# A decoder layer on one NeuronCore: the shared expert's pieces spread anew over three stretches, and the experts begun two slots sooner

## The chip, the core and the metric

The kernel runs on one NeuronCore of a Trainium2 chip. Its engines each work through a queue of their own, in order: TensorE (PE) multiplies matrices into PSUM, VectorE (DVE) and ScalarE (ACT) work on tiles in SBUF and read PSUM, GpSimd (POOL) works on tiles and issues indirect DMAs, SyncE (SP) issues ordinary DMAs, and 16 DMA engines carry them out. They meet only through semaphores. The metric is device time of one launch in microseconds; smaller is better. The run used for the profile has a time of its own, which stands beside the median of the other runs below.

## What is computed

One decoder layer on x of shape (32, 256, 256), all in float32. Self-attention with 16 heads of 16 and a layer norm; cross-attention to a context of 120 rows, each head the difference of two softmaxes, and a layer norm; then a mixture of experts on the 8192 tokens, whose result is added to the tokens and normalised again. The part that matters here is the last:

```python
scores = jax.nn.sigmoid(x @ router_weight.T)                # 64 experts
_, top_idx = jax.lax.top_k(scores + expert_bias, 6)
# each expert takes at most CAP = 96 of its tokens, in order
hmid = gelu(einsum('ech,ehf->ecf', xs, w1))                 # 256 -> 128
y = einsum('ecf,efh->ech', hmid, w2)                        # 128 -> 256
out = zeros.at[token_of].add(y_pair)                        # weighted, scattered back
shared = gelu(x @ sw1.T) @ sw2.T                            # 256 -> 512 -> 256, every token
x = layernorm(x + out + shared)
```

The routed experts see at most 64 x 96 rows. The shared expert sees every token.

## The kernel before

**Two stages.** In the first, the 32 batch entries go through both attentions, the router and the dispatch, software-pipelined: every step of a batch entry has a place in a table (`plan`), keyed by an iteration number and a part of it (`pre`, `mm`, `post`), and line 1121's loop runs the iterations. The last step of a batch entry (`dispatch`, line 1070) scatters its token rows, by 12 indirect DMAs of POOL, to the DRAM buffer `slots`, where each expert has 96 rows. Ahead of it stand on PE `router` and `places` (line 1036, two small products that count the tokens ahead of each), and on DVE `route`, `keys` and `slots_of` (line 1060). For the last entries the steps lie closer: `router` in iteration 18 after the entry's cross-attention began, `places` in iteration 20, the dispatches from 21 to 25. `store` puts each entry's normalised tokens in DRAM twice: transposed in `x2T_d`, and as the start of `acc[0]`; `acc[1]` is cleared.

In the second stage (from line 1138) the 64 experts are taken as 32 pairs. A loop over slots emits the work; pair n has its number n = slot - START. In slot n PE transposes the pair's rows (`turn`), one slot on it does the first product (`up`), and another slot on the second (`down`). In the slot after that DVE weights the result into one of six tiles `ye` and POOL issues two indirect DMAs that add it to DRAM (`scatter`, line 1229): the first expert of the pair into `acc[0]`, the second into `acc[1]`. Two scatters into the same `acc` are not in flight together: the later one waits for the earlier one to land. The rows of the next pairs (`rows_of`, eight tiles `xs`) and their weights (`expert_weights`, ten tiles `four`) are loaded by SP as tiles come free: the rows of pair m wait for the `ye` of pair m - 8.

After the experts come the 16 blocks of 512 tokens (`Last`, line 1252), one step each: `fetch` loads both `acc`, `add` sums them on POOL, `stats` adds the shared expert's `y` on DVE and takes mean and variance, `scale` makes the factors on ACT and POOL, `put` normalises on ACT and stores. The engines' queues hold these parts in the order in which the loop emits them. The first `fetch` waits until every scatter has landed.

**The shared expert's pieces.** `shared` (line 242) is a Python generator. Each `next(pieces)` emits one piece and stops. After an opening piece that loads weights, there are four pieces for each block k: two that multiply block k with half of `sw1` each (call them f), with a gelu on ACT after each, and two that multiply block k - 1's gelu with `sw2` (call them q), each followed by a copy on ACT into the tile `y` of block k - 1. That is 64 pieces of work in all, in the order f f q q. What reads a piece's PSUM is held in `unread` and emitted by `settle()` at the next piece, so a gelu or copy stands on ACT's queue behind whatever was emitted in between. PSUM in the second stage has two double banks for f and four single banks for q and for the pairs (`Apart`, line 213). The loads of a block's tokens (`load`, line 245, four tiles `x2T`) are emitted on SP three blocks ahead.

Pieces are emitted in four stretches. In the first stage, one `next` at line 1125 and one in each of the iterations named on line 1131, counted from the start of the last entry's cross-attention. In the second, one in each slot before START, then in the slots in which line 1339 says so, and from END = START + 32 + 3 on one in each slot, two in each fourth slot:

```python
            if slot < START or slot < END and n % 3 < 2:
                pieces_on(1)
            elif slot >= END:
                pieces_on(1 if slot % 4 else 2)
            if slot >= END and (not 2 <= steps < NBLK + 2 or steps - 2 in whole):
```

The last line means that the step with block k's `stats` is emitted only once both q pieces of block k, and their copies, have been.

The first EARLY blocks keep their `y` in a tile of their own in the pool `ffn`, which is there in both stages (line 261). The other blocks' `y` lie in `ypool`, which is opened in the second stage over memory that the first stage used, so their first writes wait for the last readers of that memory; so do the first loads of weights and rows. At START - 2 the rows of the first six pairs are asked for, and in slot 1 their weights.

The order on each engine's queue is the order of emission (`InOrder`, line 163, writes it down as dependencies), so a piece emitted between two other steps is done between them.

Of the kernel before, what the change touches and what calls it, by code (L numbers as in the profile page):

```python
# [37 lines left out]
def tile_decoder_layer(  # L38
# [24 lines left out]
    B, T, _ = x.shape  # L63
# [167 lines left out]

    NQ = TB // P
    NBLK = NT // TB
    EARLY = min(3, NBLK)
    ys, whole, unread = {}, set(), []

    def settle():

        while unread:
            unread.pop()()  # L240

    def shared(ypool):
# [15 lines left out]
        def keep(k, q2, ps):  # L258
            if q2 == 0:
                tag = "y" if k >= EARLY else f"y{k}"  # L260
                bufs = None if k >= EARLY else 1
                ys[k] = ypool(k).tile([P, NQ, D], F32, tag=tag, name=tag, bufs=bufs)
# [59 lines left out]
    with ExitStack() as one:  # L322
# [777 lines left out]
        batches = [Batch(b) for b in range(B)]  # L1100
        ypools = []
        pieces = shared(lambda k: ypools[0] if k >= EARLY else ffns[0])

        def run(n, part):
            for _, f, args in sorted(plan.pop((n, part), ()), key=lambda step: step[0]):
                f(*args)

        def score_products(k):

            pairs = []  # L1110
            for kind, behind in ((Batch.weights, 10), (Batch.maxima, 0)):
                for bt in batches:
                    if any(0 <= k - 2 * t - behind < 8 for t in (bt.start, bt.cross)):
                        pairs.append(kind(bt, k))
            for n in range(2):
                for mms, _ in pairs:
                    for dst, lhsT, rhs in mms[2 * n : 2 * n + 2]:
                        pe.matmul(dst, lhsT=lhsT, rhs=rhs, start=True, stop=True)
            return [read for _, read in pairs]

        for n in range(min(plan)[0], max(plan)[0] + 1):
            if n == batches[-1].start + 13:
                early_end.close()
                ffns.append(ctx.enter_context(tc.tile_pool(name="ffn", bufs=2, side="right")))
                next(pieces)
            run(n, "pre")
            settle()
            for read in score_products(2 * n) + score_products(2 * n + 1):
                read()
            run(n, "mm")  # L1130
            if n - batches[-1].cross in (-5, -1, 3, 7, 9, 10, 11, 12, 13, 14, 15, 16, 17, 18, 19, 20):
                next(pieces)
            run(n, "post")
        settle()
# [3 lines left out]
    with ExitStack() as two:  # L1138
# [4 lines left out]
        small = two.enter_context(tc.tile_pool(name="small2", bufs=3))  # L1143
        ypool = two.enter_context(tc.tile_pool(name="ypool", bufs=NBLK - EARLY - 1))
        ypools.append(ypool)
        AHEAD = 6
        START = 7

        fours = itertools.count()

# [4 lines left out]
        def rows_of(n):  # L1155

            xs = wk.tile([CAP, 2, XPW], F32, name=f"xs{n % 8}", bufs=1)
            sp.dma_start(
                out=xs,
                in_=slots[2 * n * CAP : (2 * n + 2) * CAP, :].rearrange("(e s) d -> s e d", s=CAP),  # L1160
            )
            return xs

        def tokens_of(n):

            code = xs_of[n][:, :, D + NE]
            empty = small.tile([CAP, 2], F32, tag="empty", name="empty")
            dve.tensor_scalar(empty, code, 0.0, slot_f[:CAP, :], ALU.is_equal, ALU.mult)
            token = small.tile([CAP, 2], F32, tag="token", name="token")
            dve.tensor_scalar(token, code, -1.0, float(NT), ALU.mult, ALU.add)  # L1170
            idx = small.tile([CAP, 2], I32, name=f"idx{n % 12}", bufs=1)
            dve.tensor_add(idx, token, empty)
            return idx

        def expert_weights(n):

            wt = next_four([P, 2, D // P * F + D])
            sp.dma_start(out=wt, in_=w12[n])
            return wt
# [125 lines left out]
        last = [Last(k) for k in range(NBLK)]  # L1305
        END = START + NP + 3
        slot = steps = 0
        more = True

        def pieces_on(n):  # L1310
            nonlocal more
            for _ in range(n):
                if more:
                    more = next(pieces, "end") != "end"

        def fetch_for(n):
            if n < NP:
                xs_of[n] = rows_of(n)
                weights_of[n] = expert_weights(n)

        while more or steps < NBLK + 5:
            n = slot - START

            if 0 <= n - 1 < NP:
                pairs[n - 1].turned()
            if 0 <= n - 2 < NP:
                pairs[n - 2].gelu()
            if 0 <= n - 3 < NP:
                pairs[n - 3].scatter()
            if slot == 1:  # L1330
                for k in range(AHEAD):
                    weights_of[k] = expert_weights(k)
            if slot == START - 2:
                for k in range(AHEAD):
                    xs_of[k] = rows_of(k)
            if 0 <= n < NP:
                idx_of[n] = tokens_of(n)

            if slot < START or slot < END and n % 3 < 2:
                pieces_on(1)  # L1340
            elif slot >= END:
                pieces_on(1 if slot % 4 else 2)
            if slot >= END and (not 2 <= steps < NBLK + 2 or steps - 2 in whole):
                for part, behind in (
                    (Last.fetch, 0),
                    (Last.add, 1),
                    (Last.scale, 3),
                    (Last.put, 4),
                    (Last.stats, 2),
                ):  # L1350
                    if 0 <= steps - behind < NBLK:
                        part(last[steps - behind])
                steps += 1
            if 0 <= n < NP:
                pairs[n].turn()
            if 0 <= n - 1 < NP:
                pairs[n - 1].up()
            if 0 <= n - 2 < NP:
                pairs[n - 2].down()
                fetch_for(n - 2 + AHEAD)  # L1360
            slot += 1
# [62 lines left out]
```

## Time and profile before

| | |
|---|---|
| median of 7 runs | 1932.17 us (1929.36 to 1939.80) |
| the profiled execution's own time | 1926.0 us |
| its span, first to last instruction | 1924.3 us |
| granted TensorE clock, mean | 0.979 |

The busy time by stretches, from the trace, in us:

| stretch | PE | DVE | ACT | POOL | DMA engines, mean share |
|---|---|---|---|---|---|
| 0 to 1600: first stage but for its end | 1530.37 | 1118.19 | 938.73 | 985.75 | 0.15 |
| 1600 to 1643: end of the first stage | 41.01 | 13.74 | 16.55 | 34.58 | 0.17 |
| 1643 to 1671: up to the first scatter | 26.32 | 4.07 | 10.60 | 3.44 | 0.85 |
| 1671 to 1848: the pairs of experts | 167.70 | 52.23 | 40.70 | 90.18 | 0.69 |
| 1848 to 1924: the 16 blocks | 34.54 | 53.00 | 51.13 | 58.91 | 0.86 |

A stretch of 1643 to 1671 is 28 us long, so PE's 26.32 there means that it hardly paused. All instructions carry line 173, that of a helper, so tiles tell them apart: `two<-x2T,w_s` is an f piece (8 matmul instructions), `one<-w_s,gT` a q piece (16), `one<-ident,xs` the transposes of a pair, `one<-xsT,four` its first product, `one<-four,hT` its second, `acc<-ye,idx` a scatter, `slots<-xpt,slot` a dispatch.

In an engine's lines in order of time the columns are start and duration in us, engine, line, operation, written and read tiles with their shapes, how many instructions were merged, and in brackets the idle time of the engine before it and what is taken to have ended it. That last is inferred from semaphores and can name the wrong one.

### The profile page before, as it was taken

The numbers are of one execution on the slowest core, as the hardware profiler recorded it, in microseconds if no ns is written. First come the engines' busy times: TensorE is split into PE (matmuls) and PEld (weight loads), VectorE is DVE, ScalarE is ACT, GpSimd is POOL, SyncE is SP. The second block draws the span as 40 slices with busy tenths as digits, with TensorE's granted clock in tenths as the row PEclk, the third lists the DMA queues.
The fourth block names the chain that finished last, engine by engine and source line by source line (L and its number), as shares of the span: only waits on it lengthen the run. The fifth ranks groups of instructions, "written<-read, shape, count | busy, mean of one in ns | idle before, by whom it ended". The sixth has DMA issues, their size and how long they took to land. (4 is left out here: it accounts for less than half of the span.)

```text
span 1924.3 us, 44465 instructions
## 1 busy us (share of the span) xinstructions
PE 1799.9 (94%) x17800; PEld 1316.7 (68%) x17800; DVE 1241.2 (65%) x2749; ACT 1057.7 (55%) x1807; POOL 1172.9 (61%) x1242
## 2 busy tenths in 40 slices
PE   7999999999999999999999999999999879998973
PEld 4777777777777776777777777777777556676642
DVE  5566677777777777777777777777777534133246
ACT  1666666655556665555666655555666554222237
POOL 7444445666666666666666666666445658344567
PEclk9999999999999999999999999999999889999987
DMA  3070111111111111111111111111012012787477
GB/s 114 15 193 7 32 31 59 63 45 44 38 35 37 35 34 35 35 37 35 35 34 32 33 32 33 32 33 33 22 31 85 19 56 57 206 224 202 85 233 308
DMA packets 109550, 132.14 MB, mean 69 GB/s; under 512 B 33019, under 2 KB 94676, under 8 KB 109344
## 3 DMA queue, kind: packets, MB, share of 16 engines
q1 hardware_dynamic: 78832, 106.83, 17.9%
q0 software_dynamic: 25600, 13.02, 4.1%
q10 hardware_dynamic: 4912, 9.46, 1.3%
q8 instruction: 140, 2.29, 0.5%
q14 instruction: 66, 0.54, 0.1%
HBM read 74.62 MB, written 111.04 MB: 96 GB/s over the span
## 5 line engine op out<-in xcount | busy, mean ns | idle before, releaser
L173 DVE TENSOR_REDUCE pad_mx<-all 128x4 f32<-128x1024 f32 (+1 forms) x512 | 586.9, 1187 | 277.8 <-PE all L173 277.4
L173 ACT ACTIVATE pt<-all 128x512 f32<-128x512 f32 (+3 forms) x768 | 516.8, 740 | 273.9 <-PE all L173 216.8
L173 PE MATMUL all<-qT,kT 32*128 32x256 f32 (+1 forms) x4096 | 518.7, 390 | 37.7 <-POOL qT L173 34.7
L173 PE MATMUL all<-kT,qT 32*128 32x256 f32 (+1 forms) x4096 | 511.1, 388 | 5.1 <-DVE qkb L173 2.9
L173 PEld LDWEIGHTS all<-qT,kT 32*128 32x128 f32 (+1 forms) x4096 | 363.4, 182 | 162.0 <-issue 71.1
L173 POOL DMA_INDIRECT slots<-xpt,slot x384 | 385.4, 1004 | 95.0 <-issue 91.3
L173 PEld LDWEIGHTS all<-kT,qT 32*128 32x128 f32 x4096 | 365.9, 186 | 17.6 <-DVE qkb L173 3.3
L173 POOL TENSOR_TENSOR qT<-qT,mT 128x512 f32<-128x512 f32 x126 | 159.1, 1283 | 222.7 <-ACT mT L173 222.7
L173 PE MATMUL all<-w_qkv,xT 128*128 128x512 f32 (+1 forms) x512 | 184.1, 494 | 8.6 <-DMA xT<-in_xT 8.6
L173 ACT COPY ot<-all 128x512 f32<-128x512 f32 x192 | 112.1, 589 | 95.7 <-PE all L173 85.4
L173 POOL DMA_INDIRECT acc<-ye,idx x64 | 90.2, 1409 | 107.2 <-DMA acc<-ye,idx 33.9
L173 POOL TENSOR_SCALAR rs<-mv 128x2 f32<-128x2 f32 x64 | 14.2, 222 | 190.4 <-DVE mv L173 190.0
L173 PEld LDWEIGHTS all<-w_qkv,xT 128*128 128x128 f32 x512 | 94.1, 194 | 51.4 <-issue 43.9
L173 ACT COPY T<-all 128x512 f32<-128x512 f32 x128 | 73.1, 591 | 91.2 <-PE all L173 88.0
L173 PE MATMUL all<-pt,pad_xv 120*32 120x256 f32 x2048 | 119.1, 384 | 2.9 <-ACT pt L173 2.8
L173 PE MATMUL all<-pt,pad_v 128*32 128x256 f32 x2048 | 117.1, 381 | 0.0
L173 POOL TENSOR_TENSOR rc<-qkb,cosr 128x512 f32<-128x512 f32 x62 | 79.9, 1289 | 47.4 <-DVE qkb L173 46.4
L173 POOL TENSOR_TENSOR pad_qk<-rc,qkb 128x256 f32<-128x256 f32 x124 | 102.2, 845 | 2.7
L173 PE MATMUL all<-ident,ot 128*128 128x128 f32 x768 | 103.5, 278 | 0.0
L173 PE MATMUL one<-w_s,gT 128*128 128x256 f32 x416 | 95.0, 384 | 5.4 <-ACT gT L173 2.4
L173 PEld LDWEIGHTS all<-ident,ot 128*128 128x128 f32 x768 | 84.0, 142 | 21.4 <-ACT pt L173 13.4
L173 PEld LDWEIGHTS all<-pt,pad_xv 120*32 120x32 f32 x2048 | 63.5, 111 | 48.8 <-issue 6.8
(155 smaller groups left out, 2921.8 us busy)
## 6 DMA issues: line engine op xcount, KB each, us to landing
four<-in_w SPq DMA_DIRECT2D x32, 512.0 KB, 5.0
four<-acc SPq DMA_DIRECT2D x32, 512.0 KB, 6.2
xT<-in_xT SPq DMA_DIRECT2D x32, 256.0 KB, 3.5
xt<-in_x SPq DMA_DIRECT2D x32, 256.0 KB, 4.3
x2T_d<-T SPq DMA_DIRECT2D x32, 256.0 KB, 2.5
acc<-xpt SPq DMA_DIRECT2D x32, 256.0 KB, 2.6
acc<-zero SPq DMA_DIRECT2D x32, 256.0 KB, 3.1
x2T<-x2T_d SPq DMA_DIRECT2D x16, 512.0 KB, 6.3
```

Of the source, the lines that this page charges most:

```text
L173: ins = f(*args, **kwargs)
```

## The change

Four numbers and one condition change. EARLY goes from 3 to 4, so block 3's `y` gets a tile in `ffn`, and `ypool` has 11 tiles, not 12. In the first stage, iterations 17 to 20 take two pieces each, not one: 20 in place of 16. START goes from 7 to 5: five pieces, not seven, stand ahead of the first pair's slot, and the rows of the first pairs are asked for in slot 3, not 5. Between START and END a piece is emitted in each third slot (12 pieces), not in two of three (24). What is left, 28 calls in place of 18, comes from END on.

```diff
-    EARLY = min(3, NBLK)
+    EARLY = min(4, NBLK)
...
-            if n - batches[-1].cross in (-5, -1, 3, 7, 9, 10, 11, 12, 13, 14, 15, 16, 17, 18, 19, 20):
+            for _ in range(
+                (-5, -1, 3, 7, 9, 10, 11, 12, 13, 14, 15, 16, 17, 17, 18, 18, 19, 19, 20, 20).count(
+                    n - batches[-1].cross
+                )
+            ):
                 next(pieces)
...
-        START = 7
+        START = 5
...
-            if slot < START or slot < END and n % 3 < 2:
+            if slot < START or slot < END and n % 3 == 0:
                 pieces_on(1)
             elif slot >= END:
                 pieces_on(1 if slot % 4 else 2)
```

## The prediction

> **What bounds the kernel now.** The change touches the last 325 us, so I began with the busy times by stretches and then read each engine's lines in order of time. Two stretches of the pairs, whose columns are stretch, length, busy time and instruction count of PE, weight loads, DVE, ACT and POOL, then clock, DMA share and GB/s:
>
> ```profile
> 1671.00:1797.00 126.00, 116.70 (x619) 88.49 (x619) 44.08 (x152) 27.32 (x42) 59.21 (x42) 0.97 0.78 201
> 1797.00:1848.00 51.00, 51.00 (x217) 36.03 (x216) 8.15 (x25) 13.38 (x14) 30.97 (x22) 1.00 0.46 65
> ```
>
> POOL's instructions here are only scatters: 42 in the first 126.0 us (6.00 us a pair), 22 in the next 51. PE looks full, and the chain that ended last begins its way through the pairs with PE:
>
> ```profile
> DMA acc<-ye,idx 5%; PE one L173 3%; PE two L173 1%; POOL four L173 1%; DMA four<-acc 1%; POOL rstd L173 0%; DMA four<-in_w 0%; DVE ye L173 0%; ACT four L173 0%; POOL acc L173 0%; DVE y L173 0%; POOL slots L173 0%; SPq L173 0%; DVE st L173 0%; POOL off L173 0%
> ```
>
> Is PE the bound? I matched pairs to scatters. Pair 2's result was weighted here, and its first scatter went here:
>
> ```profile
> 1680.81 0.87 DVE L173 TENSOR_SCALAR ye<-one,xs 96x256 f32<-96x256 f32 x2 [1.20 <-PE one L173]
> ...
> 1684.27 1.41 POOL L173 DMA_INDIRECT acc<-ye,idx  x1 [4.18 <-DVE idx L173]
> ```
>
> The tile was ready at 1681.7; the scatter went 2.6 us later, although POOL was idle. It is the fifth scatter, and the third (1676.97, also into the first accumulator) had to land. By 1735 PE has done pair 15's second product while POOL is at pair 11; from 1766 PE itself stops, since the six `ye` tiles are taken. So the scatters are the bound from the second pair on, not PE. Without loads beside them they run at 4.10 us a pair (pairs 26 to 30 begin at 1818.84 to 1835.24: 16.40 / 4).
>
> After the last scatter the end is set by the queues. ACT meets block 0's `scale` and stops; the gelus behind it stop PE:
>
> ```profile
> 1857.76 0.30 ACT L173 ACTIVATE rs<-mv,eps 128x4 f32<-128x4 f32 x1 [20.94 <-DVE mv L173]
> ...
> 1845.02 3.60 PE L173 MATMUL two<-x2T,w_s 128*128 128x512 f32 x8
> 1860.05 5.54 PE L173 MATMUL two<-x2T,w_s 128*128 128x512 f32 x8 [11.43 <-ACT gT L173]
> 1865.42 7.07 PE L173 MATMUL one<-w_s,gT 128*128 128x256 f32 x32
> 1872.33 7.37 PE L173 MATMUL two<-x2T,w_s 128*128 128x512 f32 x16
> 1879.54 7.07 PE L173 MATMUL one<-w_s,gT 128*128 128x256 f32 x32
> 1887.01 1.13 PE L173 MATMUL one<-w_s,gT 128*128 128x256 f32 x4 [0.40 <-ACT gT L173]
> 1888.82 6.31 PE L173 MATMUL one<-w_s,gT 128*128 128x256 f32 x28 [0.68 <-ACT rs L173]
> ```
>
> Nine pieces are left when ACT goes on; they end at 1895.13, some 29 us before the end, while ACT and POOL work on with little pause.
>
> **Part 1, the start of the pairs.** A piece costs 3.44 us of PE back to back (1824.34 to 1831.25 is two: 6.91). Four more in the first stage are 13.8 us; PE had its last piece there at 1627.21, so it now ends at 1644.4, not 1630.65. Six pieces, not eight, then stand ahead of the first `turn`: 20.7 us, so PE is ready at 1665.1. But three of the four added pieces (iterations 17, 18, 19) stand ahead of the last entry's `places`: 10.3 us. These lines show what hangs on that:
>
> ```profile
> 1628.66 0.42 DVE L173 TENSOR_SCALAR slot<-top 128x16 int32<-128x16 f32 x1
> ...
> 1631.99 0.99 POOL L173 DMA_INDIRECT slots<-xpt,slot  x1 [0.16 <-issue]
> ...
> 1646.24 0.97 POOL L173 DMA_INDIRECT slots<-xpt,slot  x1 [0.30 <-issue]
> ...
> 1652.03 2.80 SPq L173 DMA_DIRECT2D xs<-slots  x6
> ...
> 1662.40 0.49 PE L173 MATMUL one<-ident,xs 96*128 96x96 f32 x4
> ```
>
> The slots come at 1629.08 + 10.3 = 1639.4, the dispatches begin 7.4 us later than 1631.99 and, POOL being back to back, end 7.4 later. So do the weights, which SP asked for at 1643.54 behind POOL's last fence, and the rows: 1659.4, usable (1657.11 before) at 1664.5. PE's 1665.1 covers that by 0.6 us; without this cover the delay would be up to 7.4. The router's gelu and route lie earlier than `places` by 3 us or more and are hidden. The first `turn` moves by +2.7; the 8.6 us from it to the first scatter at 1671.01 lose the one piece in between (3.44). First scatter: -0.8, with bounds -3.5 (no delay of `turn`) and +7.4 (the rows late by all of it). The copy of block 3's `y` no longer waits for old memory, but block 4's waits there instead: nothing.
>
> **Part 2, among the pairs.** Twelve fewer pieces take 12 x 3.44 = 41 us from PE. PE is not the bound, so I cost this at nothing. PE now needs 2.09 us for a pair (1680.60 to 1682.69) and 3.44 / 3 for a piece, 3.24 a slot, and will stand idle behind the `ye` tiles sooner. What speeds the scatters is less traffic. The 21 pairs up to 1797.13 took 126.1 us, 40.0 more than 21 x 4.10. In that time SP issued 24 loads of a pair (240.8 + 512 KB) and five `x2T` (512 KB), 20.6 MB: 1.94 us for a MB. Three `x2T` loads (blocks 13 to 15) move behind the last scatter: two of 1.0 us, and one that stretched pair 23 to 5.22 us, 1.1. Together -3.1. No row shows scatters with PE running this far ahead. Bound on the slow side: pairs 16 to 20, with PE already held by `ye`, took 31.61 / 5 = 6.32 us against 6.00, over 21 pairs +6.7. On the fast side: pairs 12 to 14 took 14.26 / 3 = 4.75, which over 21 pairs is -26. I take -3.1, since the other loads stay the same.
>
> The row says that PE also slows after a pause: behind 5.29 us of idle at 1783.9 the four products took 2.02 us, not 1.03, and the piece after them 5.08, not 3.62. The Trainium skill, "TensorE: Matmul & The Clock Gate" (section "HAM oscillation — how this bites in real kernels"), warns of idle gaps of more than about 3.4 us, after which the clock falls to half. This speaks against the change: at half clock throughout, by that page's figure, a slot would need 6.5 us, above the scatters' pace, some 26 us over the last 11 pairs.
>
> I cost the pauses at nothing, because a slot's own idle share is some 2 to 3 us and PE stands several pairs ahead.
>
> **Part 3, after the pairs.** ACT's stop comes as before, 14.6 us after the last scatter's issue, since the steps begin two slots sooner but wait for the same landing. PE again gets nine pieces in ahead of it: emission order puts five copies and gelus ahead of the first `scale`, and two double banks and four single ones let four more pieces be computed. But 27 pieces follow the last `down`, not 18. So 18 remain, not 9. The nine took 1860.05 to 1895.13, 35.1 us, 3.90 each with the slow first ones. Eighteen take 70.2: 1860.05 - 0.8 - 3.1 + 70.2 = 1926.4. Now the last q piece ends late and block 15 hangs on it: copy 0.6, ACT's `scale` and `put` of blocks ahead of it 6.8 in all, during which DVE's 3.5 and POOL's 1.3 are hidden, its own `put` 2.1, and 3.7 from its store's issue to the end (1920.60 to 1924.3). That is 13.2, so the span ends at 1939.6, +15.3. Block 13's load now stands on SP behind the first `fetch`, lands early in the step loop, and is needed some eight pieces on: hidden.
>
> Bounds: at 3.44 a piece the 18 take 61.9, and the sum is +7.0. ACT alone gains five gelus (1.94) and five copies (0.59), 12.7 us in a stretch that it works through without a break until 1907, less about 2.7 of waits in its last three blocks: +10, inside that. If PE and ACT, both near full, hold each other up by half a piece in each of the five added blocks' worth of steps, 9 us more: +24.
>
> **Sum.** -0.8 - 3.1 + 19.2 = +15.3 on 1924.3. Its own time of 1926.0 becomes 1941. The runs' median lies 6.2 above that execution; I put the difference on the median: 1947.5. This outcome's own range is 1937 to 1957.
>
> **Rivals.** *The scatters run free* (faster). The chain names PE up to 1735; if thinning PE's work and bunching the loads early lets the 21 loaded pairs run like the late ones, 40 us go and 19.2 come: 1932.2 - 0.8 - 40 + 19.2 = 1911. It decides from 0.9 us a pair on. Against it: `ye` ready early while POOL waits, and the same loads to be made. 0.14. *The added pieces hide* (no change): PE stands idle for 29 us at the end, and if ACT's gaps take the gelus, only parts 1 and 2 count, 1928, or up to 1937 with part of ACT's 10. Against it: 31 us more PE work in a gap that begins only with the stop. 0.17. *Held scatters* (slower still): the held pace of 6.32 and the late rows both come true: +19.2 + 6.7 + 7.4 = +33, 1965. For it: the 0.6 us of cover. 0.14. The forecast has 0.55. That pieces are simply not moved is excluded by counting them: 20, 5, 12 and 27 make 64.
>
> **Range and chances.** Taking in the hidden case and the most of the held one, 1929 to 1960. About 0.3%, 5.8 us, can be told from no change. Faster: 0.14. Same: the hidden case and a little of the forecast's low end, 0.18. Slower: 0.68.
>
> **What would show it.** The last dispatch near 1654 and the first scatter within 3 us of 1671; loaded pairs still at 5.8 to 6.3 us; PE idle among the pairs; the last q piece near 1926 and the chain of waits ending through it into block 15's `stats`. A pace below 5.1 us a pair would make me wrong; so would a last q piece before 1912.

## The result, and the profile after

| | before | after |
|---|---|---|
| median of the runs | 1930.57 us (46 runs, 1922.66 to 1943.12) | 1947.81 us (19 runs, 1942.50 to 1951.85) |
| ratio, 95% interval | | 1.0085 [1.0073, 1.0097] |
| profiled execution, its span | 1924.3 us | 1943.4 us |

The change makes the kernel 0.85% slower; the forecast was 1947.5 us. The moments along the path that sets the end show where the 19.1 us between the two spans lie (start times of the lines, us):

| | before | after | forecast shift | shift |
|---|---|---|---|---|
| last entry's `places` on PE | 1626.77 | 1636.10 | +10.3 | +9.3 |
| last dispatch | 1646.24 | 1653.17 | +7.4 | +6.9 |
| rows asked for by SP | 1652.03 | 1659.24 | +7.4 | +7.2 |
| first `turn` | 1662.40 | 1666.41 | +2.7 | +4.0 |
| first scatter | 1671.01 | 1672.18 | -0.8 | +1.2 |
| last scatter | 1843.15 | 1846.42 | -3.9 | +3.3 |
| ACT's stop (first `rs`) | 1857.76 | 1861.20 | -3.9 | +3.4 |
| PE goes on behind the stop | 1860.05 | 1863.97 | -3.9 | +3.9 |
| last q piece ends | 1895.13 | 1930.56 | +31.3 | +35.4 |
| end of the span | 1924.3 | 1943.4 | +15.3 | +19.1 |

**The start of the pairs.** PE's lines of the changed kernel in order of time, from the last pieces of the first stage to the first `turn`; the bracket holds the idle time ahead of the line:

```profile
1636.10 0.38 PE L173 MATMUL all<-sel,before_it 128*128 128x128 f32 x2
...
1636.54 7.03 PE L173 MATMUL all<-x2T,w_s 128*128 128x512 f32 x16
1645.63 7.17 PE L173 MATMUL one<-w_s,gT 128*128 128x256 f32 x32 [2.05 <-ACT gT L173]
1652.64 7.03 PE L173 MATMUL two<-x2T,w_s 128*128 128x512 f32 x16
1659.51 7.07 PE L173 MATMUL one<-w_s,gT 128*128 128x256 f32 x32
1666.41 0.82 PE L173 MATMUL one<-ident,xs 96*128 96x96 f32 x8
```

Two pieces end the first stage, six stand ahead of the `turn`, as counted. Between them lie 2.05 us in which PE waits for ACT's gelu of the last f piece.

**The pairs.** The busy time in the two stretches that were shown of before, cut at this kernel's own pairs (stretch, length, busy time and count of PE, weight loads, DVE, ACT, POOL, then clock, DMA share, GB/s):

```profile
1672.18:1802.00 129.82, 103.60 (x528) 78.36 (x528) 43.80 (x151) 17.83 (x34) 59.21 (x42) 0.83 0.72 188
1802.00:1851.00 49.00, 46.32 (x191) 32.33 (x190) 7.71 (x24) 10.66 (x11) 30.97 (x22) 1.00 0.44 57
```

POOL's 42 scatters of 21 pairs take 129.82 us, 6.18 a pair, where they took 126.0. PE is now idle for 26 us of it, against 9 before: less work on PE bought no time here. The page's line on the chain that ended last no longer goes through PE in the pairs, but through the landing of the scatters, 8% of the span:

```profile
PE all L173 47%; POOL slots L173 10%; DMA acc<-ye,idx 8%; POOL qT L173 4%; POOL rc L173 3%; POOL qkb L173 3%; POOL x L173 2%; POOL pad_qk L173 1%; PE one L173 1%; ACT pt L173 1%; PE two L173 1%; POOL rstd L173 1%; POOL at L173 1%; DMA four<-acc 1%; POOL off L173 0%
```

The page's costliest groups name another culprit for POOL's idle time (busy, mean ns of one, idle ahead of it and its releaser):

```profile
L173 POOL DMA_INDIRECT acc<-ye,idx x64 | 90.2, 1409 | 103.5 <-DVE ye L173 40.9
```

That is a releaser to distrust. DVE's lines in the held stretch, and then POOL's:

```profile
1739.82 0.87 DVE L173 TENSOR_SCALAR ye<-one,xs 96x256 f32<-96x256 f32 x2 [4.04 <-DMA acc<-ye,idx]
...
1747.02 0.87 DVE L173 TENSOR_SCALAR ye<-one,xs 96x256 f32<-96x256 f32 x2 [5.47 <-DMA acc<-ye,idx]
```

```profile
1734.66 1.41 POOL L173 DMA_INDIRECT acc<-ye,idx  x1 [4.64 <-DVE ye L173]
1736.37 1.41 POOL L173 DMA_INDIRECT acc<-ye,idx  x1 [0.30 <-issue]
1740.44 1.41 POOL L173 DMA_INDIRECT acc<-ye,idx  x1 [2.66 <-DVE ye L173]
1742.15 1.41 POOL L173 DMA_INDIRECT acc<-ye,idx  x1 [0.30 <-issue]
1747.64 1.41 POOL L173 DMA_INDIRECT acc<-ye,idx  x1 [4.08 <-DVE ye L173]
```

Counting both lists from the first pair on, the `ye` at 1739.82 is pair 15's and the scatter at 1740.44 is pair 10's second: its tile has been ready for 31 us. What both waited for is one event, the landing of the scatter of 1734.66, pair 9's second. The chain that ended last, in order of time (start, length, what ran), shows that landing and the next two:

```profile
1734.66 5.04 DMA acc<-ye,idx
1740.44 6.46 DMA acc<-ye,idx
1747.64 5.21 DMA acc<-ye,idx
```

The landing frees pair 9's `ye` tile for pair 15, and it lets the next add into `acc[1]` go. The pace of the pairs is that landing and some 0.7 us to POOL's next line. The landing times in the trace, which come from the semaphores, say the same of all pairs: in this kernel and in the one before alike, 60 of the 62 scatters from the third on start less than 0.9 us behind the landing of their predecessor in the same `acc`, or less than 1.8 us behind the start of the scatter ahead of them on POOL. From 1815 to 1835, with little loading beside them, the same landing takes 3.3 to 3.4 us and a pair 4.1.

**The end.** ACT's stop, and PE's lines behind it:

```profile
1861.20 0.30 ACT L173 ACTIVATE rs<-mv,eps 128x4 f32<-128x4 f32 x1 [27.19 <-DVE mv L173]
```

```profile
1863.97 6.49 PE L173 MATMUL two<-x2T,w_s 128*128 128x512 f32 x8 [13.36 <-ACT gT L173]
1870.88 3.70 PE L173 MATMUL two<-x2T,w_s 128*128 128x512 f32 x8 [0.42 <-ACT rs L173]
1874.42 7.07 PE L173 MATMUL one<-w_s,gT 128*128 128x256 f32 x32
1881.91 7.13 PE L173 MATMUL two<-x2T,w_s 128*128 128x512 f32 x16 [0.42 <-ACT gT L173]
...
1909.72 7.03 PE L173 MATMUL two<-x2T,w_s 128*128 128x512 f32 x16
1916.58 13.98 PE L173 MATMUL one<-w_s,gT 128*128 128x256 f32 x64
```

An f piece is 8 instructions and a q piece 16, so 18 pieces stand here, where there were nine. PE works through them with 0.84 us of pause behind the first, and the last ends at 1930.56. The chain that ended last, in order of time (start, length, what ran), goes through them into the last block's normalisation:

```profile
1902.97 6.91 PE one L173 x32
1909.88 6.87 PE two L173 x16
1916.75 13.83 PE one L173 x64
1935.20 1.97 ACT four L173 x4
1937.63 2.07 ACT four L173 x4
```

### The profile page after: what moved, and what is told of

The parts are those of the page before. It is cut to its first block, busy times and chain, and to the rows that moved or that the text cites. A ratio compares the mean times of both kernels' runs of the same rounds, so it can differ in the third digit from the quotient of the medians.

```text
span 1943.4 us, 44472 instructions
## 1 busy us (share of the span) xinstructions
PE 1815.3 (93%) x17800; PEld 1324.9 (68%) x17800; DVE 1240.2 (64%) x2749; ACT 1057.5 (54%) x1807; POOL 1173.8 (60%) x1242
## 4 chain that ended last, share of the span: by engine, by line
PE 50%; POOL 27%; issue 10%; DMA 9%; ACT 3%; DVE 1%; POOLq 0%; SPq 0%; ACTq 0%; DVEq 0%
PE all L173 47%; POOL slots L173 10%; DMA acc<-ye,idx 8%; POOL qT L173 4%; POOL rc L173 3%; POOL qkb L173 3%; POOL x L173 2%; POOL pad_qk L173 1%; PE one L173 1%; ACT pt L173 1%; PE two L173 1%; POOL rstd L173 1%; POOL at L173 1%; DMA four<-acc 1%; POOL off L173 0%
## 5 line engine op out<-in xcount | busy, mean ns | idle before, releaser
L173 PEld LDWEIGHTS all<-pt,pad_v 128*32 128x32 f32 x2048 | 63.3, 110 | 44.0 <-ACT pt L173 5.4
```

The source lines that it names most:

```text
L173: ins = f(*args, **kwargs)
```

## The experiments

The experiments ran on three chips, and each result stands beside runs of the kernel before on its own chip. The second chip, that of the kernels without weight loads, with repeated products (the first time), without the sum and with plan pieces, had a longer first stage: the last `places` came 52 to 57 us later than in the same or the nearest kernel elsewhere (median of before: 1994.31 us); of those kernels, lengths of stages are compared, not moments. "Stretch" is the time from the first to the last scatter's issue.

**One part alone: the thinning.** The kernel before, with

```diff
-            if slot < START or slot < END and n % 3 < 2:
+            if slot < START or slot < END and n % 3 == 0:
```

> Only the thinning among the experts (one piece in three slots), with 16 pieces in the first stage and START at 7 as before. Theory: PE is not the bound among the pairs, so the first to the last scatter still take 171 to 176 us; twelve more pieces come behind the last pair, 21 are left when ACT goes on behind its stop, and the end lies 21 x 3.70 + 12.8 us behind the first of them. 27 us slower than before, some 1957 us (1950 to 1963). Rival (PE is the bound among the pairs, as the chain of waits says): the scatters take 150 us or less, and the time is at most 7 us above that of before.

Measured: 1955.16 us, 1.0102 [1.0058, 1.0146] of before; span 1956.8. Against the median of before on this chip, 1937.36, that is 17.8 us and not the 27 expected. The stretch was 175.57 us, so a PE with less to do did not let the scatters run at their free pace. The pieces behind the stop, 21 of them, end at 1944.01, and from there it is 12.8 us to the end, as in the changed kernel: PE's queue sets the end. They take 82.6 us, 3.93 each, with some 5 us of waits for ACT, in a kernel whose blocks also have the slow adds described below. The thinning by itself is a loss.

**One part alone: four more pieces in the first stage.** The kernel before with EARLY 4 and the longer list of iterations.

> Only the twenty pieces in the first stage, with their tile for block 3 (EARLY 4); START at 7 and two pieces in three slots as before. Theory: eight pieces stand between the end of the first stage and the first turn, which comes some 10.8 us later than before (1673), and so does the first scatter; the stretch of scatters keeps its 172 us; behind ACT's stop 5 pieces are left, not 9, but PE did not set the end there, so only two gelus and two copies of ACT are saved, 5 us. 5 to 11 us slower than before, 1936 to 1942 us. Rival (the pieces behind the pairs set the end in the kernel before too): four pieces fewer save 4 x 3.7 = 15 us there, and the time is 4 us below that of before.

Measured: 1947.83 us, 1.0065 [1.0026, 1.0105]; span 1944.4. The first scatter moved to 1682.08, +11 as expected, but the end moved by 20. The last piece ends at 1894.22, long before the end, so pieces are not the reason. The blocks themselves are slower: from the stop to the end 78 us, where before took 66.5. DVE's and then POOL's lines of this kernel among the blocks:

```profile
1894.56 2.28 DVE L173 TENSOR_TENSOR y<-y,four 128x1024 f32<-128x1024 f32 x1
...
1899.09 2.56 DVE L173 TENSOR_TENSOR y<-y,four 128x1024 f32<-128x1024 f32 x1
```

```profile
1893.42 2.34 POOL L173 TENSOR_TENSOR four<-four,four 128x1024 f32<-128x1024 f32 x1
1895.72 2.00 POOL L173 TENSOR_TENSOR rstd<-rs,mhalf 128x4 f32<-128x4 f32 x1
1897.80 0.20 POOL L173 TENSOR_TENSOR off<-off,rstd 128x4 f32<-128x4 f32 x1
1898.23 2.34 POOL L173 TENSOR_TENSOR four<-four,four 128x1024 f32<-128x1024 f32 x1 [0.23 <-DMA four<-acc]
```

The same two engines in the kernel before:

```profile
1896.34 1.22 DVE L173 TENSOR_TENSOR y<-y,four 128x1024 f32<-128x1024 f32 x1
...
1899.96 1.23 DVE L173 TENSOR_TENSOR y<-y,four 128x1024 f32<-128x1024 f32 x1
```

```profile
1893.96 2.35 POOL L173 TENSOR_TENSOR four<-four,four 128x1024 f32<-128x1024 f32 x1
1896.27 1.01 POOL L173 TENSOR_TENSOR rstd<-rs,mhalf 128x4 f32<-128x4 f32 x1
```

In the kernel before, DVE's add of `y` begins when POOL's sum has ended (1896.31), and takes 1.22 us. Here it begins at 1894.56, while POOL's sum runs to 1895.76, and ends 1.08 us after that: this fits an add that stood still until the sum was over. POOL's `rstd`, begun at 1895.72, then takes 2.00 us and not 1.01, and ends 0.9 us after DVE's add. A block takes 4.53 us (1894.56 to 1899.09), not 3.62, and since DVE's add then starts early again beside the next sum, the pattern seems to feed itself. The Trainium skill, "SBUF — State Buffer" (section "Who interferes with whom"), states that a VectorE instruction with two inputs in SBUF contends with a GpSimd instruction that reads SBUF, and calls the ports that the two share an exclusive lock; these lines agree, with 2.28 us against 1.22. In the thinned kernel above the same happened, with `rstd` at 1.87 us in the mean; in the changed kernel itself it did not, with the add of `y` at 1.23. Nor need every execution of one kernel have it: of the six runs here the fastest took 1933.31 us, 12.8 less than the profiled one, which is about what the slow blocks cost. No profile of that run shows whether they are the reason.

**That contention, without POOL's sum.** The kernel of the last experiment, with the sum of the two `acc` left out (so the second experts' share is not in the result):

```diff
             def add(self):
-                pool.tensor_add(self.sums[0], self.sums[0], self.sums[1])
+                pass
```

> The kernel with only the twenty pieces of the first stage (START 7, two in three slots), in which POOL's sum of the two accumulators is left out, so the second experts' share is missing in the output. In its parent DVE's y additions took 2.2 us each and POOL's powers 1.9, against 1.23 and 1.06 in the other kernels, and a block took 4.54 us. Theory (DVE's addition and POOL's addition, when they overlap, hold each other up): without POOL's addition the y additions take 1.23 us throughout and a block 3.6 us or less. Rival (the y additions are slow for a reason of their own, such as the traffic of the DMA engines): they stay at 2.2 us and the block at 4.5.

Measured in a single run: the add of `y` takes 1.19 to 1.23 us in all 16 blocks, `rstd` 1.14 in the mean, and from the stop to the end it is 64.9 us, 13 fewer. The slow form is gone with the sum, though one run alone would prove little, since most kernels that have the sum don't show it either. With the lines above it speaks for the overlap with the sum as the cause. What tips an execution into it is open.

**One part alone: START.** The kernel before with START 5 in place of 7, run on two chips.

> Only START at 5, with 16 pieces in the first stage and two pieces in three slots as before. Theory: the rows are there at 1657.6 and PE is ready before that, so the first turn moves from 1662.4 to about 1657.6 and the first scatter from 1671 to 1666; the stretch of scatters keeps its 172 us; 11 pieces are left behind ACT's stop, which the idle time of PE at the end covers. 5 us faster than before, 1924 to 1928 us. Rival (the traffic, not the start, decides when the last scatter lands): no change.

> The kernel before with START 5 alone, a second time. Theory: first turn 6 us sooner than in the kernel before, last piece ends 15 us or more ahead of the end and doesn't set it; 0.988 to 0.995 of the kernel before (0.9913 the first time). Rival (the first result was a lucky chip): 0.997 to 1.003.

Measured: 1916.79 us, 0.9913 [0.9879, 0.9947], and on the other chip 1920.92 us, 0.9936 [0.9915, 0.9958]. It beats both kernels. PE's line of its first `turn` in the first of the two:

```profile
1656.13 0.52 PE L173 MATMUL one<-ident,xs 96*128 96x96 f32 x4 [1.54 <-DMA xs<-slots]
```

The `turn` comes 6.3 us sooner than before and now waits 1.54 us for the rows, so all that pieces ahead of it can give has been taken. The last piece ends at 1896.39, 20 us before the end: the two pieces moved behind the pairs are hidden there. One of them gets in ahead of ACT's stop, so that ten stand behind it, where eleven were expected. The medians moved by 14 and 21 us and the spans by 5.1 to 7.8 against the one profile of before, which in its own time lay 9 to 11 us under before's medians on these chips; the six of the `turn` are shown, the remainder of the medians' gain is not explained.

**The change without the thinning,** on two chips: the changed kernel with `n % 3 < 2`.

> The changed kernel with only the thinning undone (two pieces in three slots again; 20 pieces in the first stage, START 5). Theory: the first scatter lies one piece later than in the changed kernel, 1675 to 1676, the stretch of scatters takes 171 to 176 us, 6 or 7 pieces are left behind ACT's stop and no longer set the end. 1 to 6 us slower than before, 1931 to 1937 us: nearly all the loss is in the thinning. Rival (the late dispatch and the earlier START cost the time): it stays above 1943 us.

> The changed kernel with two pieces in three slots again, a second time. Theory: stretch of the scatters 166 to 170 us (166.31 the first time), 5 us or more under the changed kernel's on the same chip, and 0.995 to 1.000 of the kernel before. Rival: the stretch lies within 3 us of the changed kernel's; the time is still under it by 10 us or more, since the last piece no longer sets the end.

Measured: 1929.30 us, 0.9974 [0.9950, 0.9998], and 1931.38 us, 0.9988 [0.9968, 1.0007]. In the first of them PE's last lines behind the stop are:

```profile
1871.81 7.07 PE L173 MATMUL one<-w_s,gT 128*128 128x256 f32 x32
1879.31 1.13 PE L173 MATMUL one<-w_s,gT 128*128 128x256 f32 x4 [0.43 <-ACT gT L173]
1881.11 6.31 PE L173 MATMUL one<-w_s,gT 128*128 128x256 f32 x28 [0.67 <-ACT rs L173]
```

PE is done at 1887.42, 37 us before the end. So the other three edits together are worth little, and the thinning carries the loss. The expectation of 1 to 6 us slower than before missed, since the stretch was 166.31 us and not 171 to 176.

**The changed kernel again,** beside the last, on the same chip.

> The changed kernel once more, beside its variants on one chip, to see how far the stretch from first to last scatter (174.24 us in its first profile) varies between executions. Theory (thinning the pieces lets PE run ahead and be held by the six ye tiles, which makes the scatters slower): again 173 to 177 us. Rival (the stretch wanders by some 5 us from one execution to the next, whatever the pieces do): anything from 166 to 177. Both: 1.0085 of the kernel before, pieces behind the stop at 3.5 to 4.0 us each.

Measured: 1946.87 us, 1.0073 [1.0049, 1.0097]. Against the kernel without thinning on this chip that is 15.5 us (1946.87 - 1931.38). The pieces behind the stop take 66.7 us, 3.70 each. The stretch is 173.79 us, against 174.24 the first time, and 3.9 us longer than without thinning on this chip (169.93), between the 5 us of the theory there and the 3 of its rival.

**What the weight loads cost the scatters.** The changed kernel without the weight loads of 512 KB behind the first six pairs: the later pairs use the weights of those six, so their results differ. By the count of DMA issues that is 26 loads of the 32; in the changed kernel 24 of them were issued from the first scatter on.

```diff
-                weights_of[n] = expert_weights(n)
+                weights_of[n] = weights_of[n % AHEAD]
```

> The changed kernel with the weights of the pairs from the seventh on left out: each takes the tile of one of the first six pairs, so the experts' values are others, and 24 loads of 512 KB are not made. Theory (the loads, MB by MB, are what stretches the scatters beyond 4.10 us a pair): 12.6 of 20 MB are gone; at 2.2 us a MB the first 21 pairs take 86 + 7.4 x 2.2 = 102 us, 4.9 a pair, where the changed kernel took 129.8, 6.18 a pair; first to last scatter some 147 us, not 174. Rival (PE's pauses and its half clock set the pace of the pairs in the changed kernel): the pace stays at 6 us a pair or more.

Measured in a single run: stretch 146.17 us, 4.81 a pair in the first 21. The busy time of that stretch of 21 pairs:

```profile
1726.15:1827.23 101.08, 89.71 (x526) 70.36 (x526) 43.88 (x151) 17.82 (x34) 59.26 (x43) 0.97 0.60 115
```

PE does the same work (526 instructions against 528), and POOL the same scatters, in 101.08 us and not 129.82. So the weight loads hold the pairs, at 174.24 - 146.17 = 28.1 us for 24 x 0.524 = 12.6 MB: 2.2 us for a MB. The changed kernel itself has no profile on this chip; the other stretches measured on it are 168.61 to 176.10 us.

**Does a PE that runs ahead slow the scatters?** The changed kernel, with the first product of each third pair done five times, which gives PE work without a piece's loads and gelu; on two chips.

```diff
-                for k, e in enumerate(self.es):
+                again = 5 if self.n % 3 == 0 else 1
+                for k, e in [ke for _ in range(again) for ke in enumerate(self.es)]:
```

> The changed kernel, in which the first product of each third pair is computed five times over, into the same place: 3.5 us of PE work with no use, in the slots where the thinning took a piece away. No load, no copy and no piece is added. Theory (a PE that runs ahead and is then held by the ye tiles puts the loads right behind the landings, where they meet the next scatters; a slower PE does not): the stretch from first to last scatter falls from 174 us to 164 to 168, though PE has more to do; the first scatter comes some 3.4 us later, and the end 3 to 6 us earlier than in the changed kernel. Rival (PE's work among the pairs makes no difference to the scatters; what differed between the thinned kernels and the others was something else): 174 us, and the end 3 us later than in the changed kernel.

> The changed kernel with the first product of each third pair done five times, so that PE has the missing work without ACT's and the loads' part of a piece. Theory: stretch 165 to 170 us, near the one with two pieces in three, and a time 3 to 7 us under the changed kernel's, since the last piece moves with the scatters. Rival: 173 to 177 us, no nearer to that than the changed kernel itself, and the same time as it within 0.3%.

Measured: 1998.92 us, 1.0015 [0.9989, 1.0042], and 1944.71 us, 1.0050 [1.0028, 1.0071]. The stretch is 168.61 and 166.22 us, in the theory's range both times. In time the second lies 2.2 us under the changed kernel on its chip, where 3 to 7 were expected, with overlapping intervals. All stretches in one table:

| kernel | pieces in three slots | stretch, us |
|---|---|---|
| after, twice | 1 | 174.24, 173.79 |
| thinning alone | 1 | 175.57 |
| after with repeated products, twice | 1 | 168.61, 166.22 |
| before | 2 | 172.14 |
| after without thinning, twice | 2 | 166.31, 169.93 |
| START alone, twice | 2 | 169.91, 174.28 |
| four more pieces in the first stage; also without the sum | 2 | 169.51, 170.48 |
| pieces put into the plan (next) | 2 | 176.10 |

Three profiles of thinned kernels lie at 173.8 to 175.6, and work on PE brings two down. But the same kernel, START alone, gives 169.91 and 174.28, and one with two pieces in three slots gives 176.10. The wandering of 4 us and more is as large as the difference, so both the theory and its rival stay possible. What the table does exclude is that thinning shortens the stretch by anything like 40 us.

**Pieces where PE has a gap.** START 5, two pieces in three slots, EARLY 4, the old list of 16, and two more pieces as steps of the plan, seven iterations after the last entry's cross-attention began:

```diff
+        for _ in range(2):
+            plan.setdefault((batches[-1].cross + 7, "mm"), []).append((1, next, (pieces,)))
```

> A version meant to be faster: START at 5, two pieces in three slots, and two more pieces in the first stage (18), placed where PE stands idle for 9.1 us at 1555 to 1564, ahead of the transposes that wait for POOL; block 3's y in a tile of its own. Theory: the two pieces hide in that gap, the last places come no later than with START 5 alone (1627.6), first turn at 1656, first scatter at 1665, the stretch 168 to 170 us, nine pieces are left behind ACT's stop; 1 to 3 us faster than with START 5 alone, 0.985 to 0.991 of before. Rival (what PE does there is waited for by something else): places and the last dispatch come up to 7 us later, and the time is that of before or a little less.

Measured: 1978.85 us, 0.9926 [0.9898, 0.9953]. The last `places` stands at 1679.32, where the kernels with the longer list had it at 1690 to 1693 on this chip, and PE had been idle for 9.18 us ahead of it, waiting for DVE: on this chip, pieces placed there do not delay the dispatch. But the ratio is that of START alone, so the two more early pieces bring nothing to be seen, and its stretch was the longest of all.

## Why the prediction was right, and where its steps were off

**The mechanism held.** Next to nothing changed among the pairs, nine more pieces came to stand behind ACT's stop, and the last q piece came to set the end: each was forecast, and each is in the lines above. The kernel without thinning puts a price on it: 15.5 us on one chip, for which the forecast's two terms (-3.1 among the pairs, +19.2 behind them) gave 16.1.

**The sum held in part by errors that cancel.** That 1947.5 lies 0.3 us from the measured median is luck: between the two profiles the change is 19.1 us and not 15.3, between the medians 17.2, and the median of before came down from 1932.17 to 1930.57 with more runs. Parts one and two were to give -3.9 up to the last scatter and gave +3.3; part three was to give +19.2 and gave 15.2 (66.6 + 12.84 from PE's first piece behind the stop to the end, against 64.25 before), and 0.65 more lies around the stop.

- *First `turn`, +2.7, measured +4.0.* The step that failed is "PE is ready at 1665.1". Pieces were put back to back, and the wait for the gelu at the change of stages, 2.05 us, was left out, though PE's lines of before have one too, of 1.99 us. The delay of the dispatch, +7.4, was 6.9, and PE covered the rows as forecast.
- *From the first `turn` to the first scatter, 5.2 us by the forecast, 5.8 measured.* One piece left that stretch, as counted. In the START experiments, where that piece stays, the distance is 8.6 us as before; the `turn` comes 6.3 and 6.5 us sooner there, since nothing delays the dispatch.
- *The pairs, -3.1, measured +2.1.* The mis-sized term is "Three `x2T` loads move behind the last scatter". A price of 1.94 us for a MB of traffic is about right for weights (2.2 by the run without them). The part that lay on pair 23 came: that pair took 4.34 us, not 5.22. The other two loads left the 21 loaded pairs as well, three `x2T` loads in place of five, and these pairs took 3.7 us longer. In none of the three profiles of thinned kernels without the repeated products is the stretch shorter than in the one of before. The forecast's two bounds for the pace, 4.75 and 6.32 us a pair, held: 6.18 and 6.15. Whether PE held by the `ye` tiles makes up for the loads taken away is what the table of stretches leaves open.
- *PE's pauses, cost nothing.* They came: the granted clock over the loaded pairs fell from 0.97 to 0.83. PE's line of a q piece among them, which takes 3.44 us in a row of such pieces at full clock:

```profile
1753.90 5.23 PE L173 MATMUL one<-w_s,gT 128*128 128x256 f32 x16 [1.34 <-DVE ye L173]
```

  In the same stretch each `ye` waits for a landing and not for PE, so no slowed product is on the path. The Trainium skill's warning of a clock at half after idle gaps of more than about 3.4 us ("TensorE: Matmul & The Clock Gate", section "HAM oscillation — how this bites in real kernels") came true in the clock and not in the time; here slowed products also stand behind pauses of only 1.3 to 2.6 us, as in this line.
- *Eighteen pieces at 3.90 us, measured 3.70.* The nine of before held one slow first piece and 1.08 us of waits; the forecast spread these over 18 as if they recurred. They came once: 18 x 3.44 = 61.9, and 4.7 us of start and pauses make 66.6. That PE and ACT hold each other up among the added pieces, the upper bound, did not happen: 0.84 us in all.
- *12.84 us from the last piece to the end, forecast 13.2.*

**The rivals.** That the scatters run free fell with a stretch of 174 us where it needed some 132. That the added pieces hide fell with the chain through them to the end; it holds in the START kernel, for two pieces moved behind the pairs, one of them behind the stop, and not for nine. Of the held scatters, the pace came true by about half, +3.7 of +6.7 over the 21 loaded pairs (+2.1 up to the last scatter), and the late rows cost nothing, since PE's own work covered them.

**What the forecast did not see** is that one of the edits is a gain by itself. Part one of the forecast was costed as a whole, -0.8 at the first scatter, with the `turn` and the rows worked out apart; the same working without the four more pieces has PE ready at 1651.3 and the rows at 1657.11, so a first `turn` some 5 us sooner; START alone showed 6.3. That its medians gained more than that, 14 and 21 us, no working here explains.

## What to carry to other kernels

Before work is moved off an engine that looks full, match what it makes with what consumes it: where results lie ready for 30 us, the engine's fullness is not the bound, and the work comes back at the end, where nothing hides it. Count the pieces that land behind the last stop and compare their time with the idle time of that engine there: nine fitted into 64 us of blocks, and ten with START alone; eighteen did not. When several numbers change at once, cost each alone, since one of them may be the whole gain and another the whole loss.

## What was not expected of the hardware

- Two elementwise adds on two engines, DVE's of 128x1024 and POOL's of 128x1024, seem to hold each other up when they overlap (2.28 us for DVE's and not 1.22), and the overlap can repeat block after block: 4.53 us a block and not 3.62, some 12 us over the 16 blocks. It showed in two of the profiles here and not in the others, with the same instructions in the same order on each of the two queues.
- A releaser in the profile can be a fellow sufferer: POOL's wait was put down to DVE's `ye`, and both had waited for one landing, 5.04 us behind its issue.
- A scatter of 96 rows of 1 KB that adds to DRAM lands 3.3 to 3.4 us after its issue with little beside it and mostly 3.7 to 7.5 us with loads beside it, 5.0 in the mean over the 42 of the loaded pairs, and a chain of such adds runs at that pace and some 0.7 us from a landing to the next start.
